# Attention values two units to a bank, and layer 3 with gelu and tanh read straight from PSUM

## The chip, the cores and the metric

One Trainium2 chip, one of its cores. The metric is the device time of one execution in microseconds (us); of a kernel's runs the median is taken. Three runs of the kernel before took 2492.44, 2498.31 and 2498.45 us.

## The reference

Four layers are applied one after the other to x, which holds 4 batches of 512 tokens with 512 channels in float32. A conditioning vector of 512 numbers per batch scales and shifts the normalised activations. Cut to what matters:

```python
# layer 0: layernorm, 16 heads of 32 with windowed keys from a latent, projection
# layer 1: rms norm, 8 query heads of 64 over one key head; then a gated MLP of 2048
# layer 2: layernorm, 16 heads of 32, normalised q and k; then an MLP of 2048 with tanh-gelu
# layer 3, eight experts of 64 channels each, side by side:
xr = x.reshape(Bx, Tx, 8, 64)
h = jax.nn.gelu(jnp.einsum('btel,elf->btef', xr, W1) + b1, approximate=False)
y = (jnp.einsum('btef,efl->btel', h, W2) + b2).reshape(Bx, Tx, Dx)
hn = _layernorm(y, ln_g, ln_b) * (1.0 + scale) + shift
return x + jax.nn.silu(hn) @ out_W + out_b
```

In each attention layer the scores pass a softmax and are then multiplied by the values.

## The kernel before, in words

All matmuls are float32. The kernel's author writes stages as Python generators and runs two of them side by side: side A (`AttentionSide`, line 427) and side M (`OtherSide`, line 463). A stage is a kind and a batch: `a01` is the attention of layers 0 and 1, `a2` that of layer 2, `m1` the MLP of layer 1, `m2` the MLP of layer 2 followed by layer 3, `mlp2` that MLP alone, and `half0` and `half1` are layer 3 for tokens 0 to 255 and 256 to 511 of the last batch. The lists `STREAM_A` and `STREAM_M` (line 98) say which stage each side takes in which order. At the start both sides have an `a01`; from then on an attention stage of one batch stands beside an MLP stage of another; at the end `half1` is left alone.

The order of the instructions is set before the program runs, by a planner. `Clocks` (line 161) keeps a model of when every tile is written and every engine is free. A stage yields `Until(...)` when its next piece needs something; `interleave` (line 1576) picks, among the pieces whose wait is over by the model, the one whose stage is furthest behind, and notes its instructions. At the end all noted instructions are emitted in the order of their modelled start. So a change of one stage's pieces moves the instructions of both sides, and nothing is reordered on the chip: each engine works through its own list and waits on semaphores.

All instructions of DVE, ACT and POOL are issued at line 301, all matmuls at line 354 (`mm`), all transposes at line 360 (`tr`). PSUM holds three pairs: two tiles of two banks each, called `two` (line 330), used for attention scores, and two single banks for each side, called `bank`. `evict` (line 376) copies a bank to SBUF on ACT or DVE, whichever the model frees first.

Attention (line 745) goes unit by unit. A unit is 128 queries of one group of heads: 16 units in layers 0 and 2, and 8 in layer 1. `scores` makes one unit's scores in two `two` tiles; DVE finds maxima, ACT exponentiates, POOL divides by the sum; `back` transposes the probabilities on PE and evicts them to `pT` tiles (side A) or `hid` (side M); `values` (lines 988, 1082 and 1220, one for each layer) multiplies them by v. The finished units wait in the list `late`:

```python
            if len(late) == 2:
                yield Until(*when, side.at, of=late[0][1])
                values(*late.pop(0))
                cost += work[1]
```

So the values of unit i-2 run when unit i is about to be transposed. Value products of layers 0 and 2 use 32 columns of the PE array and four of them run side by side in the four column groups (the profile writes the stationary shape 128*32), those of layer 1 use 64 (128*64). The scores use 32 or 64 rows (32*128, 64*128). All other large products and the transposes use the whole array (128*128).

Layer 3 is `experts` (line 1291). For each of four pairs of experts, `first` multiplies 64 channels by w1 (64*128), in two steps f of two products; after each step DVE adds the bias to one half and ACT to the other, and after both one gelu runs over the whole `hid` tile. `second` multiplies by w2 (128*64), DVE adds b2, `third` transposes back to y. Then `norm` takes mean and variance of each token's 512 values with one `bn_stats` and one `bn_aggr`, POOL raises the variance to the power -1/2, DVE scales, `turned` transposes and applies gain and lift (half the chunks on ACT, half on DVE), one silu runs over all of hT, and the products with `out3` follow.

Of the kernel before, what the change touches and what calls it, by code (L numbers as in the profile page):

```python
# [19 lines left out]
P = 128  # L20
# [288 lines left out]
def cond_seq_kernel(ctx: ExitStack, tc: tile.TileContext, a: dict, out: bass.AP):  # L309
# [17 lines left out]
    def name(s):  # L327
        return f"{s}_{next(uid)}"
# [310 lines left out]
        for _ in norm_steps(*args, **kw):  # L639
            pass  # L640

    def norm_steps(n, src, eps, rms=False, tiles=range(NT)):

        mv, own = tiny([P, NT, 2], "mv"), slice(tiles[0], tiles[-1] + 1)
        for t in tiles:
            st = tiny([P, 6], "st")
            vector.bn_stats(st, src[:, t, :])
# [97 lines left out]
    def attention(side, units, scores, back, values, work, first, final=True):  # L745

        def scorable():  # L750
            return max(locked[0], clocks.free("two", 2, 2))

        def later(rest):
            locked[0] = math.inf

            def then():
                locked[0] = 0.0
                rest()

            return then  # L760

        yield Until(scorable, of=first)
        (p, rest), late = scores(units[0]), []
        rest()
        yield work[0]
        for i, u in enumerate(units):
            cost, more = 0.0, i + 1 < len(units)
            when = [scorable] if more else []
            if len(late) == 2:
                yield Until(*when, side.at, of=late[0][1])  # L770
                values(*late.pop(0))
                cost += work[1]
            else:
                yield Until(*when)
            nxt, rest = scores(units[i + 1]) if more else (None, None)
            side.open = final and i + 2 >= len(units)

            if more:
                rest = later(rest)
            yield cost + (work[0] if more else 0.0)  # L780
            pT = yield from back(u, p, rest)
            late.append((u, pT))
            p = nxt
        for u, pT in late:
            yield Until(side.at, of=pT)
            values(u, pT)
            yield work[1]

    def turn_full(side):
        def back(u, p, then):  # L790
# [95 lines left out]
    def attention0(b, side):  # L886
# [98 lines left out]
                yield 0.45  # L985
            return [pT]

        def values(u, pT):
            c, qt = u
            (pT,), o, bl = pT, side.bank(), blocks(qt)  # L990
            for i, (at, n) in enumerate(bl):
                for g in range(4):
                    mm(
                        o[quarter(g), 0:P], lhsT=v[0:n, qt, i, quarter(g)],
                        rhs=pT[0:n, i, g * P : (g + 1) * P], start=i == 0, stop=i == len(bl) - 1,
                    )
            evict(ctxT[:, c, qt * P : (qt + 1) * P], o[:, 0:P])

        if "1" not in tabs:

# [10 lines left out]
    def attention1(b, side):  # L1011
# [67 lines left out]
            soft(0)  # L1079
            return p, lambda: soft(1)  # L1080

        def values(u, pT):
            c2, qt = u
            o = side.bank().rearrange("p (i q) -> p i q", q=P)
            for i in range(2):
                for at in range(NT):
                    for j in range(2):
                        mm(
                            o[half(j), i, :], lhsT=v[:, at, :], rhs=pT[i][:, j, at, :],
                            start=at == 0, stop=at == NT - 1,  # L1090
                        )
            evict(ctxT[:, 2 * c2 : 2 * c2 + 2, qt * P : (qt + 1) * P], o[:, 0:2, :])
# [70 lines left out]
    def attention2(b, side):  # L1163
# [9 lines left out]
        for which, dst in (("q2", qT), ("k2", kT)):  # L1173
            unit = side.ring.take(which)
            for t in range(NT):
                ps = yield from by_token(side, t, hT, unit)
                q, sq = side.t1(), side.t2()
                if which == "q2":
                    vector.tensor_tensor(q, ps, qb, ALU.add)
                else:  # L1180
                    vector.tensor_copy(q, ps)
                scalar.activation(sq, q, AF.Square)
                ss, inv = tiny([P, 16], "ss"), tiny([P, 16], "inv16")
                vector.tensor_reduce(ss, sq.rearrange("p (h d) -> p h d", d=32), axis=AX.X, op=ALU.add)
# [32 lines left out]
            soft(0)  # L1217
            return p, lambda: soft(1)

        def values(u, pT):  # L1220
            c, qt = u
            o = side.bank()
            for at in range(NT):
                for g in range(4):
                    mm(
                        o[quarter(g), 0:P], lhsT=v[:, at, c * P + 32 * g : c * P + 32 * g + 32],
                        rhs=pT[g // 2][:, g % 2, at, :], start=at == 0, stop=at == NT - 1,
                    )

            vector.tensor_scalar(ctxT[:, c, qt * P : (qt + 1) * P], o[:, 0:P], vb[:, c : c + 1], None, ALU.add)  # L1230
# [60 lines left out]
    def experts(b, side, tiles=range(NT)):  # L1291
# [11 lines left out]
        w1 = unit[:, 0:1024].rearrange("p (c f) -> p c f", f=256)  # L1303
        w2 = unit[:, 1024:2048].rearrange("p (e f l) -> p e f l", f=2, l=64)
        y = side.n()

        def first(p):
            hid = side.hid()
            per = 4 // len(hid)

            def at(j, f):
                return hid[2 * j // per][:, (2 * j + f) % per, 0:n]

            for f in range(2):
                yield Until(side.pair_at, of=[xT[:, p, lo : lo + n], w1])
                s = side.pair()
                for j in range(2):
                    r = slice(64 * j, 64 * j + 64)
                    mm(
                        s[j][:, 0:n], lhsT=w1[r, p, f * P : (f + 1) * P], rhs=xT[r, p, lo : lo + n],  # L1320
                        start=True, stop=True,
                    )
                for j in range(2):
                    bias = V_B1 + 4 * p + 2 * j + f
                    if j == 0:
                        vector.tensor_scalar(at(j, f), s[j][:, 0:n], vec[:, bias : bias + 1], None, ALU.add)
                    else:
                        scalar.activation(at(j, f), s[j][:, 0:n], AF.Identity, bias=vec[:, bias : bias + 1])
                yield 1.2 * n / S
            for h in hid:  # L1330
                scalar.activation(h[:, :, 0:n], h[:, :, 0:n], AF.Gelu)
            return at

        def second(p, at):
# [13 lines left out]
        def third(p, yT):  # L1348
            yield Until(side.at, of=[yT[:, 0:n]])
            ps = side.bank()  # L1350
            for t in range(len(tiles)):
                tr(ps[:, t * P : (t + 1) * P], yT[:, t * P : (t + 1) * P], ident)
            evict(y[:, tiles[0] : tiles[-1] + 1, p * P : (p + 1) * P], ps[:, 0:n].rearrange("p (t n) -> p t n", n=P))
            yield 0.45 * n / S

        hid = yield from first(0)
# [8 lines left out]
                t = tiles[p]  # L1365
                gpsimd.tensor_tensor(xs[b][:, t, :], xs[b][:, t, :], ob, ALU.add)
        yield from third(*late)
        norm(y, y, 1e-5, tiles=tiles)
        hT = side.late()
        yield from turned(side, y, hT, b, coefs["gain"], coefs["lift"], tiles)  # L1370
        side.open = side.clear = side is sideM
        scalar.activation(hT[:, :, lo : lo + n], hT[:, :, lo : lo + n], AF.Silu)
        for t in tiles:
            ps = yield from by_token(side, t, hT, unit3)
            if n < S:
# [16 lines left out]
    def conditioning(side):  # L1392
# [93 lines left out]
        vector.tensor_tensor(gain, e1, col(V_LNG), ALU.mult)  # L1486
        vector.tensor_tensor(lift, e1, col(V_LNB), ALU.mult)
        vector.tensor_tensor(lift, lift, coefs["e2"], ALU.add)
        yield 1.0
        bias2.append(buf("late"))  # L1490
        load(bias2[0], a["bias"].rearrange("(t p) k -> p t k", p=P))
# [197 lines left out]
```

## Time and profile before

| What | Value |
|---|---|
| runs | 2492.44, 2498.31, 2498.45 us |
| profiled execution, its own time | 2497.25 us |
| its span, first to last instruction | 2495.5 us |
| granted TensorE clock over the span | 0.992 |
| activation table loads on ACT (39) | 50.0 us |
| gelu over 128x2048 (with the silu of the full stages, 27) | 1.911 us each |
| biased copy of a bank on ACT, 128x512 | 0.681 us each |
| bias added from a bank on DVE, 128x512 | 0.746 us each |
| bn_stats over 128x512 (DVE) | 0.685 us each |

PE is TensorE's matmul row, PEld its weight loads, DVE VectorE, ACT ScalarE, POOL GpSimd. A group is written as line, engine, operation, output and inputs, shape and count. For a matmul the first shape is that of the stationary operand, so a group with 128*32 uses 32 columns of the array. Matmuls are pipelined: the length of one (0.27 us for 128 columns, 0.6 us for 512) is its latency, and what it costs in a row of many is the distance from its start to the next start.

### The profile page before, as it was taken

The numbers are of one execution on the slowest core, as the hardware profiler recorded it, in microseconds if no ns is written. First come the engines' busy times: TensorE is split into PE (matmuls) and PEld (weight loads), VectorE is DVE, ScalarE is ACT, GpSimd is POOL, SyncE is SP. The second block draws the span as 40 slices with busy tenths as digits, with TensorE's granted clock in tenths as the row PEclk, the third lists the DMA queues.
The fourth block names the chain that finished last, engine by engine and source line by source line (L and its number), as shares of the span: only waits on it lengthen the run. The fifth ranks groups of instructions, "written<-read, shape, count | busy, mean of one in ns | idle before, by whom it ended". The sixth has DMA issues, their size and how long they took to land.

```text
span 2495.5 us, 33420 instructions
## 1 busy us (share of the span) xinstructions
PE 2432.5 (97%) x12564; PEld 1242.0 (50%) x12564; DVE 1190.5 (48%) x3180; ACT 877.6 (35%) x2071; POOL 733.5 (29%) x921
## 2 busy tenths in 40 slices
PE   7989999999999999999999999999999999999997
PEld 4555655444554555554455455554455444554443
DVE  6766552133654454625554455443465333763233
ACT  2645441002551351414353043333255202651233
POOL 2433320005332223324222232424332205533221
PEclk9999999999999999999999999999999999999998
DMA  3220122220113111111211111112111221102210
GB/s 112 100 74 18 52 68 68 86 87 34 35 52 106 51 52 55 39 68 55 89 48 61 63 69 65 42 56 72 68 35 52 83 89 53 44 32 95 72 55 21
DMA packets 83312, 154.18 MB, mean 62 GB/s; under 512 B 3584, under 2 KB 10784, under 8 KB 83152
## 3 DMA queue, kind: packets, MB, share of 16 engines
q1 hardware_dynamic: 82544, 151.83, 17.9%
q8 instruction: 100, 1.64, 0.3%
q14 instruction: 60, 0.49, 0.1%
q0 software_dynamic: 176, 0.15, 0.1%
q10 hardware_dynamic: 432, 0.07, 0.0%
HBM read 147.83 MB, written 4.21 MB: 61 GB/s over the span
## 4 chain that ended last, share of the span: by engine, by line
PE 88%; DVE 3%; issue 3%; ACT 2%; POOL 2%; DMA 1%; ACTq 0%; POOLq 0%; DVEq 0%
PE bank L354 71%; PE bank L360 11%; PE two L354 6%; POOL inv L301 1%; ACT probs L301 1%; DVE probs L301 1%; ACT wm L301 0%; DVE neg L301 0%; POOL t L301 0%; DVE pT L301 0%; DMA late_ada_g<-in_units 0%; DMA wm<-in_units 0%; DVE t L301 0%; DMA late_ada_t<-in_units 0%; POOL probs L301 0%
## 5 line engine op out<-in xcount | busy, mean ns | idle before, releaser
L301 POOL TENSOR_SCALAR probs<-probs,inv 128x512 f32<-128x512 f32 (+4 forms) x544 | 316.4, 596 | 688.4 <-DVE inv L301 579.4
L301 ACT ACTIVATE probs<-probs,neg 128x512 f32<-128x512 f32 (+2 forms) x448 | 265.4, 594 | 254.8 <-DVE neg L301 254.3
L360 PEld LDWEIGHTS bank<-ident,probs 128*128 128x128 f32 (+2 forms) x1744 | 201.9, 141 | 161.9 <-issue 128.6
L360 PE MATMUL bank<-ident,probs 128*128 128x128 f32 (+2 forms) x1744 | 245.4, 276 | 4.1 <-ACT arow L301 1.2
L354 PE MATMUL bank<-mT,wm_gate 128*128 128x512 f32 x512 | 248.9, 597 | 0.0
L354 PE MATMUL bank<-mT,wm_up 128*128 128x512 f32 x512 | 245.7, 597 | 0.0
L354 PE MATMUL bank<-wm_down,hid 128*128 128x512 f32 x512 | 239.6, 596 | 0.7 <-DVE hid L301 0.7
L301 DVE CUSTOM_DVE_ANT_0 probs<-two,late 128x512 f32<-128x512 f32 x256 | 166.2, 686 | 74.3 <-PE two L354 56.4
L354 PE MATMUL bank<-wm_fc,hid 128*128 128x512 f32 x384 | 187.6, 594 | 0.0
L354 PE MATMUL bank<-mT,wm_fc 128*128 128x512 f32 x384 | 182.6, 597 | 0.0
L301 ACT COPY pT<-bank 128x512 f32<-128x512 f32 (+2 forms) x240 | 133.8, 580 | 83.8 <-PE bank L360 75.8
L354 PEld LDWEIGHTS bank<-pT,v 128*32 128x32 f32 (+2 forms) x3488 | 110.7, 116 | 95.9 <-issue 33.3
L354 PE MATMUL bank<-pT,v 128*32 128x128 f32 (+2 forms) x3488 | 146.0, 278 | 8.3 <-DVE pT L301 5.8
L301 ACT ACTIVATE mt<-bank 128x512 f32<-128x512 f32 x64 | 37.8, 591 | 327.6 <-PE bank L354 327.6
L354 PE MATMUL bank<-wa_q,h 128*128 128x512 f32 x320 | 152.4, 599 | 0.2 <-DVE t L301 0.2
L301 DVE TENSOR_TENSOR x<-x,bank 128x512 f32<-128x512 f32 x100 | 68.4, 684 | 176.1 <-PE bank L354 176.0
L354 PE MATMUL two<-kT,nq 32*128 32x512 f32 (+5 forms) x1088 | 150.0, 539 | 1.1 <-DVE mx L301 1.1
L354 PEld LDWEIGHTS bank<-wm_down,hid 128*128 128x128 f32 x512 | 91.7, 190 | 98.1 <-issue 96.2
L354 PEld LDWEIGHTS bank<-mT,wm_up 128*128 128x128 f32 x512 | 91.0, 190 | 98.2 <-issue 97.7
L301 DVE RECIPROCAL inv<-total 128x2 f32<-128x2 f32 x320 | 53.0, 166 | 172.9 <-ACT probs L301 155.7
L354 PEld LDWEIGHTS bank<-mT,wm_gate 128*128 128x128 f32 x512 | 90.0, 190 | 90.8 <-issue 90.3
L301 DVE COPY pT<-bank 128x512 f32<-128x512 f32 (+2 forms) x199 | 131.1, 680 | 5.9 <-PE bank L360 5.0
(221 smaller groups left out, 3396.3 us busy)
## 6 DMA issues: line engine op xcount, KB each, us to landing
wm_fc<-in_units SPq DMA_DIRECT2D x24, 1024.0 KB, 5.6
wm_gate<-in_units SPq DMA_DIRECT2D x16, 1024.0 KB, 5.7
wm_up<-in_units SPq DMA_DIRECT2D x16, 1024.0 KB, 5.7
wm_down<-in_units SPq DMA_DIRECT2D x16, 1024.0 KB, 5.4
wa_q<-in_units SPq DMA_DIRECT2D x10, 1024.0 KB, 5.5
wa_fc<-in_units SPq DMA_DIRECT2D x8, 1024.0 KB, 5.5
wa_o<-in_units SPq DMA_DIRECT2D x6, 1024.0 KB, 5.7
wa_k<-in_units SPq DMA_DIRECT2D x4, 1024.0 KB, 5.6
```

What stands on the lines that cost most here:

```text
L301: return call(*map(real, args), **{k: real(x) for k, x in kw.items()})
L354: latest[0] = nc.tensor.matmul(real(out), lhsT=real(lhsT), rhs=real(rhs), **kw)
L360: latest[0] = nc.tensor.transpose(real(out), real(src), unit)
```

## The change

Three things are changed.

Values: the list `late` is emptied two units at a time. One call of `values` writes both units' results beside each other into one bank, and one instruction evicts 256 columns where two evicted 128 each (twice that in layer 1). It waits for the pT tiles of both units. In the iterations between, no values run.

Layer 3: the bias is added inside the gelu, which reads PSUM directly, four times per pair of experts (each 128x512, or 128x256 in the halves). The banks come from `two`: both `two` tiles in a full stage, one in a half. Both steps f are one piece now. Each transposed chunk of y gets its `bn_stats` at once, 128 columns at a time, and `bn_aggr` reads four of them. silu(z) is written as (1 + tanh(z/2)) * z/2, with gain and lift halved beforehand: for each chunk ACT takes the tanh from the bank, DVE makes z/2 from the same bank, and DVE multiplies.

Layer 2: the copy of k's bank may go to ACT or DVE, where it was DVE's.

```diff
+    def norm_steps(n, src, eps, rms=False, tiles=range(NT), stats=None):
...
+            if stats is None:
+                st = tiny([P, 6], "st")
+                vector.bn_stats(st, src[:, t, :])
+            else:
+                st = stats[:, t, :, :]
             vector.bn_aggr(mv[:, t, :], st)
...
             if len(late) == 2:
-                yield Until(*when, side.at, of=late[0][1])
-                values(*late.pop(0))
-                cost += work[1]
+                yield Until(*when, side.at, of=late[0][1] + late[1][1])
+                values(late)
+                late = []
+                cost += 2 * work[1]
             else:
-                yield Until(*when)
+                yield Until(0.0, *when)
...
-        for u, pT in late:
-            yield Until(side.at, of=pT)
-            values(u, pT)
-            yield work[1]
+        yield Until(side.at, of=sum((pT for _, pT in late), []))
+        values(late)
+        yield len(late) * work[1]
...
+        def values(two):
+            o, (c, first) = side.bank(), two[0][0]
+            for k, ((_, qt), (pT,)) in enumerate(two):
+                bl = blocks(qt)
+                for i, (at, n) in enumerate(bl):
+                    for g in range(4):
+                        mm(
+                            o[quarter(g), k * P : (k + 1) * P], lhsT=v[0:n, qt, i, quarter(g)],
+                            rhs=pT[0:n, i, g * P : (g + 1) * P], start=i == 0, stop=i == len(bl) - 1,
+                        )
+            evict(ctxT[:, c, first * P : (first + 2) * P], o[:, 0 : 2 * P])
...
-                    vector.tensor_copy(q, ps)
+                    evict(q, ps)
...
+            yield Until(lambda: clocks.free("two", 2, 2 if n == S else 1), of=[xT[:, p, lo : lo + n], w1])
+            banks = [two_banks() for _ in range(2 if n == S else 1)]
...
+            for f in range(2):
                 for j in range(2):
                     bias = V_B1 + 4 * p + 2 * j + f
-                    if j == 0:
-                        vector.tensor_scalar(at(j, f), s[j][:, 0:n], vec[:, bias : bias + 1], None, ALU.add)
-                    else:
-                        scalar.activation(at(j, f), s[j][:, 0:n], AF.Identity, bias=vec[:, bias : bias + 1])
-                yield 1.2 * n / S
-            for h in hid:
-                scalar.activation(h[:, :, 0:n], h[:, :, 0:n], AF.Gelu)
+                    scalar.activation(at(j, f), bank(j, f), AF.Gelu, bias=vec[:, bias : bias + 1])
+            yield 2.2 * n / S
...
+            for t in tiles:
+                vector.bn_stats(stats[:, t, p, :], y[:, t, p * P : (p + 1) * P])
...
-        norm(y, y, 1e-5, tiles=tiles)
+        norm(y, y, 1e-5, tiles=tiles, stats=stats)
         hT = side.late()
-        yield from turned(side, y, hT, b, coefs["gain"], coefs["lift"], tiles)
+
+        own = slice(lo, lo + n)
+        for c in range(NC):
+            yield Until(side.at, of=[y[:, t, c * P : (c + 1) * P] for t in tiles])
+            ps, h, z = side.bank()[:, 0:n], hT[:, c, own], side.t1()[:, 0:n]
+            for i, t in enumerate(tiles):
+                tr(ps[:, i * P : (i + 1) * P], y[:, t, c * P : (c + 1) * P], ident)
+            gain, lift = (coefs[x][:, c, b : b + 1] for x in ("gain", "lift"))
+            scalar.activation(h, ps, AF.Tanh, bias=lift, scale=gain)
+            vector.tensor_scalar(z, ps, gain, lift, ALU.mult, ALU.add)
+            vector.scalar_tensor_tensor(h, h, 1.0, z, ALU.add, ALU.mult)
+            yield 0.45 * len(tiles) / NT
         side.open = side.clear = side is sideM
-        scalar.activation(hT[:, :, lo : lo + n], hT[:, :, lo : lo + n], AF.Silu)
...
+        for x in (gain, lift):
+            vector.tensor_scalar(x, x, 0.5, None, ALU.mult)
```

The `values` of layers 1 and 2 are changed in the same way as the one shown.

More of the change, by code (lines that the diff above doesn't have):

```diff
@@ L640, in norm @@
             pass
-    def norm_steps(n, src, eps, rms=False, tiles=range(NT)):
+    def norm_steps(n, src, eps, rms=False, tiles=range(NT), stats=None):
         mv, own = tiny([P, NT, 2], "mv"), slice(tiles[0], tiles[-1] + 1)
         for t in tiles:
-            st = tiny([P, 6], "st")
-            vector.bn_stats(st, src[:, t, :])
+            if stats is None:
[3 more added lines that the diff above has]
+                st = stats[:, t, :, :]
             vector.bn_aggr(mv[:, t, :], st)
@@ L986, in back @@
             return [pT]
[L988 to L997, printed above, removed]
+        def values(two):
[9 more added lines that the diff above has]
+            evict(ctxT[:, c, first * P : (first + 2) * P], o[:, 0 : 2 * P])
         if "1" not in tabs:
@@ L1080, in scores, with values @@
             return p, lambda: soft(1)
[L1082 to L1092, printed above, removed]
+        def values(two):
+            o, (c2, first) = side.bank().rearrange("p (i q) -> p i q", q=2 * P), two[0][0]
+            for k, (_, pT) in enumerate(two):
+                for i in range(2):
+                    for at in range(NT):
+                        for j in range(2):
+                            mm(
+                                o[half(j), i, k * P : (k + 1) * P], lhsT=v[:, at, :], rhs=pT[i][:, j, at, :],
+                                start=at == 0, stop=at == NT - 1,
+                            )
+            evict(ctxT[:, 2 * c2 : 2 * c2 + 2, first * P : (first + 2) * P], o)
         units = [(c2, qt) for c2 in range(2) for qt in range(NT)]
@@ L1218, in scores, with values @@
             return p, lambda: soft(1)
[L1220 to L1230, printed above, removed]
+        def values(two):
+            o, (c, first) = side.bank(), two[0][0]
+            for k, (_, pT) in enumerate(two):
+                for at in range(NT):
+                    for g in range(4):
+                        mm(
+                            o[quarter(g), k * P : (k + 1) * P],
+                            lhsT=v[:, at, c * P + 32 * g : c * P + 32 * g + 32],
+                            rhs=pT[g // 2][:, g % 2, at, :], start=at == 0, stop=at == NT - 1,
+                        )
+            rows = slice(first * P, (first + 2) * P)
+            vector.tensor_scalar(ctxT[:, c, rows], o[:, 0 : 2 * P], vb[:, c : c + 1], None, ALU.add)
         units = [(c, qt) for c in range(NC) for qt in range(NT)]
@@ L1305, in experts @@
         y = side.n()
+        if ("stats", b) not in shared:
+            shared["stats", b] = clocks.tile("stats", 1, small, (P, NT, NC, 6), "stats", name("stats"))
+        stats = shared["stats", b]
         def first(p):
@@ L1312, in at, with bank @@
                 return hid[2 * j // per][:, (2 * j + f) % per, 0:n]
+            yield Until(lambda: clocks.free("two", 2, 2 if n == S else 1), of=[xT[:, p, lo : lo + n], w1])
+            banks = [two_banks() for _ in range(2 if n == S else 1)]
+            def bank(j, f):
+                return banks[f][:, j, :] if n == S else banks[0][:, j, f * n : (f + 1) * n]
             for f in range(2):
-                yield Until(side.pair_at, of=[xT[:, p, lo : lo + n], w1])
-                s = side.pair()
                 for j in range(2):
@@ L1319, in first @@
                     mm(
-                        s[j][:, 0:n], lhsT=w1[r, p, f * P : (f + 1) * P], rhs=xT[r, p, lo : lo + n],
+                        bank(j, f), lhsT=w1[r, p, f * P : (f + 1) * P], rhs=xT[r, p, lo : lo + n],
                         start=True, stop=True,
                     )
+            for f in range(2):
                 for j in range(2):
                     bias = V_B1 + 4 * p + 2 * j + f
-                    if j == 0:
-                        vector.tensor_scalar(at(j, f), s[j][:, 0:n], vec[:, bias : bias + 1], None, ALU.add)
-                    else:
-                        scalar.activation(at(j, f), s[j][:, 0:n], AF.Identity, bias=vec[:, bias : bias + 1])
-                yield 1.2 * n / S
-            for h in hid:
-                scalar.activation(h[:, :, 0:n], h[:, :, 0:n], AF.Gelu)
+                    scalar.activation(at(j, f), bank(j, f), AF.Gelu, bias=vec[:, bias : bias + 1])
+            yield 2.2 * n / S
             return at
```

## The prediction

> **What bounds the kernel.** I read the page first (busy shares and the chain that ended last), then the busy time by stretches, then the PE timeline of one attention unit, then who PE waited for in each stretch. The page, its busy line and its chain:
>
> ```profile
> PE 2432.5 (97%) x12564; PEld 1242.0 (50%) x12564; DVE 1190.5 (48%) x3180; ACT 877.6 (35%) x2071; POOL 733.5 (29%) x921
> ...
> PE 88%; DVE 3%; issue 3%; ACT 2%; POOL 2%; DMA 1%; ACTq 0%; POOLq 0%; DVEq 0%
> ```
>
> The next view gives each stretch's length, then busy us of PE, PEld, DVE, ACT, POOL, the granted clock, DMA share and GB/s:
>
> ```profile
> 0.00:400.00 400.00, 361.95 (x2634) 217.66 (x2635) 242.54 (x786) 183.91 (x557) 131.55 (x239) 0.98 0.20 66
> 400.00:2380.00 1980.00, 1969.61 (x9587) 979.06 (x9586) 906.19 (x2314) 654.82 (x1459) 579.40 (x663) 1.00 0.18 63
> ...
> 2440.00:2495.50 55.50, 41.50 (x168) 19.17 (x166) 21.27 (x43) 20.80 (x35) 5.20 (x5) 0.84 0.07 24
> ```
>
> From 400 to 2380 us PE stands still for only 1980.0 - 1969.6 = 10.4 us: there the time is the sum of what PE does, and DVE and ACT, at 46% and 33%, only have to keep up. At the start PE idles 38 us and in the last 55 us 14 us, and there the clock is 0.84.
>
> A busy PE may still lose time between instructions, so I looked at one unit of layer 2's attention in the PE timeline (start, length, group; a float32 product makes two records, a transpose one):
>
> ```profile
> 1281.34 0.60 PE L360 MATMUL bank<-ident,probs 128*128 128x128 f32 x4
> 1281.78 1.02 PE L354 MATMUL bank<-mT,wm_gate 128*128 128x512 f32 x2
> 1282.64 0.60 PE L360 MATMUL bank<-ident,probs 128*128 128x128 f32 x4
> 1283.17 1.08 PE L354 MATMUL bank<-pT,v 128*32 128x128 f32 x32
> 1284.18 1.14 PE L354 MATMUL two<-kT,nq 32*128 32x512 f32 x8
> 1285.25 3.70 PE L354 MATMUL bank<-mT,wm_up 128*128 128x512 f32 x8
> ```
>
> Read start to start. Four transposes before a full product take 0.44 us (0.109 each), but 0.53 before the values: 0.09 is lost on leaving the 128*128 shape. The values run four side by side, 8 steps of 0.109 = 0.87, and take 1.01: 0.14 lost. The scores should take as long as one full product (0.86, from 1281.78 to 1282.64) and take 1.07: 0.21 lost. The same reading in layer 1 (1030.66, 1032.56, 1034.48 us) gives 0.15 for 128*64 values and 0.20 for 64*128 scores. So every change of PE's shape has a price, and it is paid on the engine that bounds.
>
> **Part 1, values of two units in one bank.** No matmul is added or removed: both programs have 7,674. What changes is how often the shape does. Counted in the PE order of the two built programs, by the shape that is left:
>
> - 128*128: 257 before, 206 after, at 0.093 us: 23.9 to 19.2
> - 32*128 (scores): 127 to 128, at 0.213: 27.1 to 27.3
> - 128*32 (values): 146 to 86, at 0.139: 20.3 to 12.0
> - 64*128 (scores, layer 3 first product): 69 to 50, at 0.20: 13.8 to 10.0
> - 128*64 (values, layer 3 second): 64 to 48, at 0.153: 9.8 to 7.3
>
> That is 664 changes to 519, and 94.9 to 75.8 us: **19.1 us less PE time**. (Prices are the medians of such steps over the whole trace; the rows above are instances.) By place: 3.6 us before 400 us, 13.7 from 400 to 2440, 1.8 in the tail.
>
> [...]
>
> What it costs. Values of units i-2 and i-1 now start together, right after unit i-1 was transposed, where before they ran one unit later. From the PE order, with the row times above, the PE work between a unit's last transpose and its first value product falls: the median from about 10.6 us to 6.4 in the middle, the shortest to 2.2 there and to 1.4 before 400 us. The evictions (pT copy, 0.58 us on ACT, 0.68 on DVE) end in the middle 0.7 us (median) to 2.3 (worst) after the transposes, in the start up to 3.1, as ACT's copies show. So in the middle almost all stay hidden: I add 1 us. In the start, where PE already waits for these copies,
>
> ```profile
> PE bank L354 <- DVE pT L301: 6.7, 4, 2.7
> PE bank L354 <- ACT pT L301: 3.3, 4, 1.6
> PE bank L354 <- DVE hid L301: 2.9, 3, 2.0
> ```
>
> two stages of 12 pairs each could wait. Bounds: nothing, and one DVE copy for each of 24 pairs, 24 x 0.68 = 16 us. I take 3, nearer the low end because each side's work covers the other's. Behind a waiting value product stand all later PE instructions of both sides; then scores, DVE maxima and exp come late. Fewer, wider evictions (layer 2: 64 of 0.344 us become 32 of about 0.48, the row for 128x256) save DVE 6.5 us off the path: nothing. The layer-2 k copy, now given to ACT or DVE, likewise.
>
> **Part 2, layer 3 in full stages (batches 0 to 2).** Per pair of experts, ACT did two biased copies (0.68) and a gelu over 2,048 columns (1.91), 3.3 us; now four gelus from the banks, 4 x 0.68 = 2.7. DVE loses two 0.75 adds. Chunked statistics cost DVE four short bn_stats for one of 0.685; a 128x128 DVE copy takes 0.28, so 1.1 us. silu of 2,048 columns (1.91) and its table load (1.28; 39 loads become 34) become four tanh (0.78), four more DVE scalings (0.81) and four products (0.68). All this lies beside PE in the middle; what can reach PE is order. A pair's first products now take both "two" buffers, and the next pair's wait until four gelus have read them, 2.7 us plus a table load the first time; between them PE has one second product (1.87) and four transposes (0.44). So 0.4 to 1 us can show per pair, 12 pairs: up to +8. Against that, the row
>
> ```profile
> PE bank L360 <- POOL t L301: 6.0, 4, 2.0
> ```
>
> is k or q waiting for POOL's scaling just here (1127 and 1168 us), where the new order puts other products: down to -6. I take 0.
>
> [...]
>
> **Part 3, the tail.** The last half stage is alone, and its chain is serial:
>
> ```profile
> PE bank L360 <- DVE nq L301: 3.9, 1, 3.9
> PE bank L354 <- ACT h L301: 3.1, 1, 3.1
> PE two L354 <- DVE pT L301: 1.9, 1, 1.9
> PE bank L354 <- ACT hid L301: 0.7, 1, 0.7
> ```
>
> ```profile
> 2479.11 1.28 ACT L301 ACT_TABLE_LOAD   x1 [0.49 <-DVE h L301]
> 2480.40 1.06 ACT L301 ACTIVATE h<-h 128x1024 f32<-128x1024 f32 x1
> ```
>
> The first wait spans copy, two bn_stats with aggregates (1.9 us), POOL's pow, scaling. With three of four chunks counted early, two short stats (0.28), two aggregates (0.18) and var (0.17) make 1.1: -0.8. Table load and silu, 2.34 us, go; in their place DVE does eight operations of 256 columns (0.54 and about 0.42), 3.8 us from the first transpose where the old way took 4.75 (-0.9), and PE can begin with chunk 0 (I count 0.2): -1.1. In the new PE order the last fc2 products of batch 3 stand inside the first half's chain, so its two waits (1.9, 0.7) are covered; but the last x tile must pass DVE and POOL (0.69 + 1.27) before its transpose, with little PE work between: +1.6. The last eight products took 10.1 us for 8 x 0.86, at the low clock after the waits; with a wait left I keep that. Sum -3, with its 1.8 us of shape changes -4.8; bounds 0 and -10.
>
> **Sum.** Start -3.6 + 3, middle -13.7 + 1, full stages 0, tail -4.8: -18.1. The profiled execution took 2497.25 us (span 2495.5), so 2479; the median shown, 2498.31, is 1 us above it and I take them as one.
>
> **Rivals.**
> 1. The waits eat it: the start loses the full 16 us and the full stages 8 more than I take, 2497 - 18 + 13 + 8 = 2500, no change. For: DVE runs at 61% before 400 us. Against: the stages' order leaves at least 1.4 us of cover. 0.09.
> 2. Slower: layer 3's "two" buffers. Scores of the other side use the same two buffers. If attention units ran beside the 12 pairs, each would wait four gelus (2.7 us) and PE with it: 33 us, 2479 + 33 = 2512. It decides from 7 of 12 pairs on. Against: at 1120 to 1195 us the other side does q, k and v products (wa_q, wa_k, wa_v in the timeline), no scores. 0.06.
> 3. More: the POOL waits go and the tail gains 10: 2479 - 6 - 5 = 2468 or less. 0.12.
> 4. The count falls but the price stays (a merged block refills as long as two): only part 3 is left, about 2494. Against: inside a values block the steps hold 0.109 through. 0.03.
> Forecast, 2469 to 2489: 0.70.
>
> A measurement here tells no less than 0.3% (7.5 us) from no change: faster ends at 2490.8, slower begins at 2505.8. Faster 0.70 + 0.12 = 0.82, same 0.09 + 0.03 = 0.12, slower 0.06. Range 2467 to 2490: forecast and the third case, and the near part of the first.
>
> **What would show it.** Right: 664 - 519 shape changes gone, PE busy near 2414, PE idle in the middle near 10 us, value groups of 64 records with the lost 0.14 once; no table load between the last transposes and the last products. Wrong: PE waiting for pT or hid beyond 400 us, first products of layer 3 waiting for ACT, scores waiting for layer 3's gelu.

## The result and the profile after

The kernel after took 2480.03 us (median of 6 runs, 2476.6 to 2482.74), the kernel before 2494.9 in 6 runs: ratio 0.9941, 95% interval 0.9926 to 0.9955, 14.9 us less. The forecast was 2479.0. The profiled execution took 2482.74 us, its span 2481.0; that of before took 2497.25, so the two traces differ by 14.5 us.

The page of the kernel after, its busy line and its chain:

```profile
PE 2418.9 (97%) x12564; PEld 1254.5 (51%) x12564; DVE 1177.2 (47%) x3174; ACT 856.1 (35%) x2053; POOL 737.9 (30%) x921
...
PE 91%; DVE 3%; ACT 3%; DMA 1%; issue 1%; POOL 0%; ACTq 0%; POOLq 0%; DVEq 0%
```

The number of PE records is the same, and PE is busy 13.6 us less. PE's share of the chain rose from 88% to 91%: it is still the bound.

The stretches of the kernel after (length, busy us of PE, PEld, DVE, ACT, POOL, granted clock, DMA share, GB/s):

```profile
0.00:400.00 400.00, 364.72 (x2632) 221.88 (x2633) 238.46 (x776) 184.40 (x544) 132.58 (x239) 0.95 0.20 66
400.00:2365.00 1965.00, 1954.27 (x9602) 985.93 (x9601) 903.44 (x2325) 644.30 (x1454) 582.59 (x664) 1.00 0.18 63
...
2425.00:2481.00 56.00, 43.06 (x169) 20.72 (x168) 21.62 (x53) 15.69 (x36) 7.71 (x7) 0.92 0.07 24
```

PE idles 1965.0 - 1954.3 = 10.7 us in the middle, as before. In the start it idles 35 us where it idled 38, but its clock is 0.95 where it was 0.98.

One value group of layer 2 in the PE timeline of the kernel after (start, length, group):

```profile
1278.44 2.74 PE L354 MATMUL bank<-mT,wm_up 128*128 128x512 f32 x6
1281.11 1.96 PE L354 MATMUL bank<-pT,v 128*32 128x128 f32 x64
1283.00 1.14 PE L354 MATMUL two<-kT,nq 32*128 32x512 f32 x8
```

The group now has 64 records. From its start to the next it takes 1.89 us, which is 16 steps of 0.109 and once 0.15. Before, 32 records took 1.01, with 0.14 lost: two units paid it twice.

**An account of all PE time.** I gave each product of the PE order the distance it has in an undisturbed row of its own kind (0.858, 0.432 or 0.218 us for 512, 256 or 128 columns, 0.109 for a transpose, divided by the number that run side by side), added the prediction's price at each change of shape, and called what is left of the measured distances the rest: waits, what is lost behind them, and a low clock. Stretches are cut by work done, so they hold equal work: the start is the first 340 us of products, the middle ends at 2200.

| Stretch | before: us = changes + rest | after | change predicted | measured |
|---|---|---|---|---|
| start | 423.5: 25.5 + 57.8 | 424.5: 22.0 + 62.4 | -3.6 + 3 | -3.5 + 4.6 |
| middle | 1963.0: 64.0 + 38.4 | 1945.9: 50.7 + 34.5 | -13.7 + 1 | -13.3 - 3.9 |
| tail | 94.8: 5.4 + 18.8 | 96.5: 3.1 + 22.9 | -1.8 - 3 | -2.3 + 4.1 |

The sum is -14.4 us, the difference of the two traces but for rounding. The total came out near the forecast, but from a middle that gained more and a tail that lost where a gain was expected.

The tail's waits of PE in the kernel after, 2365 us to the end (total, times, longest):

```profile
PE two L354 <- ACT hid L301: 3.2, 3, 1.9
PE bank L360 <- DVE nq L301: 2.9, 1, 2.9
PE bank L360 <- POOL x L301: 2.0, 1, 2.0
PE two L354 <- ACT pT L301: 1.8, 3, 0.6
```

The wait for nq fell from 3.9 to 2.9, the 3.1 us for the silu is gone, the x tile's wait came as expected. But the first and the last row are new: products into `two` that wait for ACT, six times, 5.0 us. The prediction had no term for them.

### The profile page after: what moved, and what is told of

It reads as the page before. It is cut to its first block, busy times and chain, and to the rows that moved or that the text cites. A ratio compares the mean times of both kernels' runs of the same rounds, so it can differ in the third digit from the quotient of the medians.

```text
span 2481.0 us, 33372 instructions
## 1 busy us (share of the span) xinstructions
PE 2418.9 (97%) x12564; PEld 1254.5 (51%) x12564; DVE 1177.2 (47%) x3174; ACT 856.1 (35%) x2053; POOL 737.9 (30%) x921
## 4 chain that ended last, share of the span: by engine, by line
PE 91%; DVE 3%; ACT 3%; DMA 1%; issue 1%; POOL 0%; ACTq 0%; POOLq 0%; DVEq 0%
PE bank L354 73%; PE bank L360 11%; PE two L354 7%; ACT probs L301 1%; DVE probs L301 1%; ACT wm L301 1%; DVE neg L301 0%; DVE mx L301 0%; DMA wa_q<-in_units 0%; DMA late_ada_s<-in_units 0%; DVE t L301 0%; DMA wm<-in_units 0%; ACT hid L301 0%; DVE wm L301 0%; DVE pT L301 0%
## 5 line engine op out<-in xcount | busy, mean ns | idle before, releaser
L301 DVE COPY pT<-bank 128x512 f32<-128x512 f32 (+2 forms) x217 | 143.0, 680 | 11.4 <-PE bank L360 10.7
L301 ACT COPY pT<-bank 128x512 f32<-128x512 f32 (+3 forms) x222 | 123.7, 581 | 67.5 <-PE bank L360 59.7
L354 PE MATMUL bank<-pT,v 128*32 128x128 f32 (+2 forms) x3488 | 131.9, 277 | 0.3 <-DVE pT L301 0.3
```

What stands on the lines that cost most here:

```text
L301: return call(*map(real, args), **{k: real(x) for k, x in kw.items()})
L354: latest[0] = nc.tensor.matmul(real(out), lhsT=real(lhsT), rhs=real(rhs), **kw)
```

## The experiments

Each run had its own runs of the kernel before beside it: 2495.23, 2493.49 and 2494.44 us in three groups of four kernels. The table has the median, its ratio to those, and the account of its profiled execution. One trace's rest can't be read closely: eight kernels with pairs have the same PE order through the start, and their rests there run from 55.6 to 62.4; three with values one by one also share an order there and have 51.9 to 57.8. In the middle the kernel after and half_two_tiles have one order, and 34.5 and 37.8.

| Kernel | us | ratio, 95% interval | changes | rest: start, middle, tail |
|---|---|---|---|---|
| before | 2494.9 | | 663 | 57.8, 38.4, 18.8 |
| after | 2480.03 | 0.9941, 0.9926 to 0.9955 | 518 | 62.4, 34.5, 22.9 |
| values_alone | 2486.99 | 0.9959, 0.9944 to 0.9975 | 568 | 61.8, 40.1, 17.0 |
| layer3_alone | 2490.04 | 0.9977, 0.9966 to 0.9987 | 613 | 55.3, 35.4, 23.1 |
| z_first | 2476.52 | 0.9922, 0.9907 to 0.9937 | 518 | 59.6, 34.2, 19.5 |
| half_two_tiles | 2470.86 | 0.99, 0.9883 to 0.9917 | 519 | 58.8, 37.8, 13.4 |
| both_mends | 2470.51 | 0.9899, 0.9885 to 0.9914 | 519 | 58.5, 35.4, 12.6 |
| two_banks_in_a_row | 2486.89 | 0.9969, 0.9957 to 0.998 | 523 | 63.4, 37.2, 22.8 |
| dummy_between_units | 2509.14 | 1.0057, 1.0045 to 1.0069 | 647 | 59.8, 37.6, 21.0 |
| dummy_behind_units | 2500.09 | 1.0022, 1.0014 to 1.0031 | 575 | 63.0, 38.7, 22.9 |
| start_one_by_one | 2472.24 | 0.9909, 0.9895 to 0.9922 | 546 | 51.9, 37.8, 15.3 |
| silu_table_back | 2472.95 | 0.9914, 0.9899 to 0.9928 | 519 | 55.8, 35.2, 17.5 |
| stats_back | 2468.33 | 0.9898, 0.9881 to 0.9916 | 521 | 55.6, 34.8, 12.3 |
| k_on_vector | 2476.37 | 0.9922, 0.9909 to 0.9936 | 519 | 61.2, 38.2, 15.7 |

### values_alone and layer3_alone: the two parts apart

The first is the kernel before with the new `late` and the three new `values`; the second is the kernel after with the old ones.

```diff
-                yield Until(*when, side.at, of=late[0][1])
-                values(*late.pop(0))
+                yield Until(*when, side.at, of=late[0][1] + late[1][1])
+                values(late)
```

> The kernel before with part 1 alone (values of two units in one bank). Theory (each change of PE's shape has its price, by the shape left): 664 changes become 568, 94.9 us become 82.5, so 12.4 us less: about 2482.5 against 2494.9. Rival (the new waits for the younger unit's pT eat it, and the gain measured lies in layer 3 and the tail): 2492 or more.

> The changed kernel with the values of each unit apart again (parts 2 and 3 alone). 664 changes of shape become 613, 88.2 us, so 6.7 us less by shapes. Theory: the layer-3 order gives back most of that in waits for ACT, since the whole change gained 14.9 and the values should account for 12.4: about 2492. Rival (layer 3 gains what the prediction gave it, 6.7 by shapes and 3 in the tail): 2485.

The values alone gained 8.2 us, the rest of the change 5.2. The first lies between its theory and its rival. For the values the account says -12.4 for 95 fewer changes, +4.0 of rest in the start, +1.7 in the middle and -1.8 in the tail: -8.5. What the 12.4 us lack is, in this trace, mostly the start. Layer 3 alone has 50 changes fewer (-6.7) and 4.3 us more rest in the tail; its median lies between theory and rival, and its profiled execution, 2489.3 us, agrees with neither better. That this part also saves changes (its two steps f are one piece) was in the prediction's count; without this run the saving would pass for one of the values.

### half_two_tiles: what the tail lost

```diff
-            yield Until(lambda: clocks.free("two", 2, 2 if n == S else 1), of=[xT[:, p, lo : lo + n], w1])
-            banks = [two_banks() for _ in range(2 if n == S else 1)]
+            yield Until(lambda: clocks.free("two", 2, 2), of=[xT[:, p, lo : lo + n], w1])
+            banks = [two_banks() for _ in range(2)]
...
-                return banks[f][:, j, :] if n == S else banks[0][:, j, f * n : (f + 1) * n]
+                return banks[f][:, j, 0:n]
```

> The changed kernel, but the half stages of layer 3 put their two steps into two tiles of two banks, as the full stages do. Theory (PE's last product of a pair waits for ACT's gelu because both use one tile): the six waits of 0.56 to 1.9 us, 5.0 us in all, go, but a pair's first products then wait for all four gelus of the pair before, some 0.3 us each: about 2477. Rival (the wait moves in full to the next pair): 2480.

It gained 9.2 us, more than either. The kernel after, PE timeline of the first pair of experts in the first half:

```profile
2409.66 1.13 PE L354 MATMUL two<-mT,wm_exp 64*128 64x256 f32 x6
2412.69 1.56 PE L354 MATMUL two<-mT,wm_exp 64*128 64x256 f32 x10 [1.90 <-ACT hid L301]
2414.18 3.68 PE L354 MATMUL bank<-wa_fc,pT 128*128 128x512 f32 x4
```

The same place with two tiles:

```profile
2409.46 1.13 PE L354 MATMUL two<-mT,wm_exp 64*128 64x256 f32 x8
2410.52 2.84 PE L354 MATMUL bank<-wa_fc,pT 128*128 128x512 f32 x6
2413.29 1.14 PE L354 MATMUL two<-mT,wm_exp 64*128 64x256 f32 x8
```

Three products (six records) run, and the fourth waits for ACT's first gelu, behind a table load of 1.28 us. In the built program that gelu stands ahead of the fourth product, and the product has a wait on it. The gelu reads the first bank of the tile and the product writes the second, so no bank is shared: the wait is kept for the tile as a whole, as I read the program. With one tile for each f there is nothing to wait for.

The waits are 5.0 us; what was lost is more. From 2409.66 to 2414.18 the eight products take 4.52 us and not 1.93 (8 x 0.216 and one change of 0.20), and the two full products behind them 1.83 and 1.78 us for 0.86 each. The clock in these four us and in the four before:

```profile
2410.00:2414.00 4.00, 2.10 (x16) 1.41 (x12) 0.00 (x0) 2.34 (x4) 3.50 (x3) 1.00 0.09 27
2414.00:2418.00 4.00, 4.00 (x8) 1.33 (x8) 0.00 (x0) 2.09 (x6) 0.00 (x0) 0.57 0.00 0
```

So a wait of 1.90 us cost 4.4: 2.6 at the wait and 1.8 behind it, at a clock of 0.57. Five more such waits, of 0.5 to 0.6 us, cost 1.2 to 1.3 each. Together 10.9 us of the tail's rest are of this kind in the kernel after, 1.2 with two tiles.

### z_first and both_mends: two engines read one bank

```diff
-            scalar.activation(h, ps, AF.Tanh, bias=lift, scale=gain)
             vector.tensor_scalar(z, ps, gain, lift, ALU.mult, ALU.add)
+            scalar.activation(h, z, AF.Tanh)
```

The second kernel has this and the two tiles of the halves.

> The changed kernel, but DVE makes z/2 from the bank first and ACT takes the tanh of that from SBUF, so that one engine alone reads the bank. Theory (two readers of one bank take turns and hold it, so the next transposes wait): the 4.6 us that transposes wait for ACT in the full stages and about 1.5 us of the last chain go: about 2474. Rival (the bank is not what is waited for, DVE is): no change, 2480.

> The kernel after with both mends of layer 3: z is made on DVE from the bank and ACT takes the tanh of z, so that only one engine reads the bank; and the halves put their two steps f into two tiles, as the full stages do. Theory (the two waits lie in different places, the bank's two readers in the last chain of each stage and the halves' shared tile in their first products, and add): 2480.0 - 3.5 - 9.2 = 2467. Rival (both mends shorten one and the same chain of the tail, and the larger hides the smaller): 2470.9, as with two tiles alone.

The prediction let z run on DVE beside the tanh on ACT. In the kernel after they take turns. ACT in a full stage, and PE, which waits for the same bank:

```profile
1156.28 2.30 ACT L301 ACTIVATE hid<-bank,coef_lift,coef_gain 128x512 f32<-128x512 f32 x3 [0.91 <-DVE mt L301]
```

```profile
1155.42 0.66 PE L360 MATMUL bank<-ident,mn 128*128 128x128 f32 x4 [1.28 <-ACT hid L301]
1157.11 0.65 PE L360 MATMUL bank<-ident,mn 128*128 128x128 f32 x4 [1.03 <-ACT hid L301]
```

ACT waits for DVE's reading (0.91 us; mt is the z of a full stage), and PE's next transposes wait until both have read (1.28 and 1.03 us). In the built program the second reader depends on the first; no run here lets the two read at once, so what that would take is not shown.

The middle's waits for these banks in the kernel after, and then with one reader:

```profile
PE bank L360 <- ACT hid L301: 4.6, 4, 1.3
```

```profile
PE bank L360 <- DVE mt L301: 3.0, 4, 1.0
```

They are 3.0 us for 4.6, and the last chain is 0.7 us shorter. The median fell by 3.5 us, nearer to the theory's number than to the rival's, but the intervals of both ratios overlap. On top of the two tiles the same edit gave 0.4 us, so the rival's number came there: the two mends do not add. In the account of z_first the middle's rest fell by only 0.3 us, the tail's by 3.4, and the start's by 2.8, though the order there is unchanged. One reader is worth between 0 and 3.5 us, and these runs don't settle where.

### two_banks_in_a_row: order or bank

```diff
-                yield Until(*when, side.at, of=late[0][1] + late[1][1])
+                yield Until(*when, lambda: side.at(2), of=late[0][1] + late[1][1])
...
-            o, (c, first) = side.bank(), two[0][0]
-            for k, (_, pT) in enumerate(two):
+            for (c, qt), pT in two:
+                o = side.bank()
```

> The kernel after, but the two units whose values run back to back go into a bank each and are evicted one by one, as before; each side has two single banks and both must now be free. The shape changes become 523, worth 76.3 us by the prediction's prices (519 and 75.8 in the kernel after), and the evictions double again in number. Theory (the gain comes from the order of the products, not from the shared bank): 2480 to 2482. Rival (the shared bank with its wider eviction is what pays, by fewer evictions and free banks): 2487 and more, as the 8 us that the values alone brought would go.

The rival's number came, within 0.1: 2486.89, 6.9 us more, so my theory that the order alone pays in full falls. What the order does alone is seen against layer3_alone, which has the same layer 3 and the old values: the middle takes 1948.6 us for 1955.7, 7.1 less, but the start 426.1 for 420.9, 5.2 more. With the shared bank the middle is the same (1945.6 to 1949.6 us in the kernel after, in z_first and in the six on two tiles), and the start takes 417.7 to 424.5 in the eight kernels named above, whose pairs share a bank. So the rival is right in the time, but the place isn't shown. The middle lies inside the range of kernels with a shared bank, which speaks for the order alone there. The start is 1.6 us above their highest and about 5 above their mean, which would fit a side that must wait for both its banks, as the edit's first lines have the planner do; but that range is 7 us wide for one and the same order. No run parts the wider eviction from the freed bank.

### dummy_between_units and dummy_behind_units: the price itself

```diff
+                if k == 0:
+                    tr(o[:, 3 * P : 4 * P], ident, ident)
```

after the inner loop over a unit's blocks; the second kernel has `k == 1`. The transposed identity goes to columns that nobody reads.

> The kernel after with one product more for each pair of units in layers 0 and 2: a 128x128 transpose of the identity into columns that nobody reads, between the first unit's values and the second's, 64 in all. It makes 647 shape changes of 519, worth 90.8 us of 75.8 by the prediction's prices. Theory (shape changes cost what the prediction says): 15.0 us for the changes and 64 x 0.109 = 7.0 for the transposes, 2480 + 22 = 2502. Rival (what costs is not the change of shape): 7 us for the transposes alone, 2487.

> The same 64 transposes, but behind the second unit's values, where a change of shape mostly follows anyway: 575 shape changes, worth 81.1 us. Theory: 5.3 us for the changes and 7.0 for the transposes, 2492. Rival (what costs is not the change of shape): 2487, the same as with the transposes between the units. The two runs differ by 10 us in the theory and by nothing in the rival.

The two hold the same 64 instructions and differ by where they stand. They differ by 9.05 us where the price of 72 changes says 9.7 and the rival nothing. So a change of shape costs about what the rows said. The PE timeline of the first kernel shows the price itself:

```profile
1291.23 1.08 PE L354 MATMUL bank<-pT,v 128*32 128x128 f32 x32
1292.24 0.33 PE L360 MATMUL bank<-ident 128*128 128x128 f32 x1
1292.50 1.08 PE L354 MATMUL bank<-pT,v 128*32 128x128 f32 x32
1293.51 1.14 PE L354 MATMUL two<-kT,nq 32*128 32x512 f32 x8
```

Each unit's values take 1.01 us again, so the 0.14 is paid twice. The level is off: the two are 7 and 8 us above the theory. The same lines hold a part of it. The lone transpose takes 0.26 us to the next product, where 0.109 and a price of 0.093 make 0.20. That is the median of all 64 in the first kernel, and of the 56 before scores in the second: 64 x 0.056 = 3.6 us, and 3.2.

The account takes the prices as given: between the units it has +15.0 for changes, +7.0 for transposes and -1.5 of rest, behind them +5.3, +7.0 and +4.9. By that rest the two profiled executions differ by only 3.3 us. The one of the first kernel took 2503.36 us, near the theory, while five others took 2507 to 2510 without a profile; where those spent it stays open.

### start_one_by_one: does it pay in the start

```diff
+            elif len(late) == 2:
+                yield Until(*when, side.at, of=late[0][1])
+                values([late.pop(0)])
+                cost += work[1]
```

for the attention of layers 0 and 1 in batches 0 and 1, on top of the two tiles in the halves.

> The kernel after with two tiles in the halves (2470.9 us), but the first two attention stages of layers 0 and 1, those of batches 0 and 1 that fill the start, take their units' values one by one as before. 546 shape changes for 519, 3.5 us more by the prediction's prices; what the start loses beyond products and changes was 57.9 us before and about 60 with the units in pairs. Theory (in the start the longer waits give back about 2.5 of the 3.5 us): 2472. Rival one (they give back more than pairs save there, so pairs don't pay in the start): 2469 or less. Rival two (pairs cost nothing in the start): 2474.5.

2472.24 against 2470.86: as the theory had it, and less than can be told from nothing. The clock from 100 to 150 us shows where the start gives back. In this kernel:

```profile
100.00:150.00 50.00, 43.50 (x493) 27.80 (x483) 37.02 (x201) 35.73 (x139) 24.34 (x60) 0.93 0.38 128
```

In the kernel after:

```profile
100.00:150.00 50.00, 43.38 (x436) 29.13 (x432) 31.16 (x175) 33.03 (x125) 21.33 (x53) 0.76 0.33 115
```

PE is busy equally long and gets fewer instructions done. On two tiles, the base of this run, the clock there is 0.87 with 472 records. Three kernels with values one by one in the start have 0.93 here; the others, with pairs, 0.73 to 0.90.

### silu_table_back, stats_back and k_on_vector: the small parts

All three stand on half_two_tiles, with one edit of the change undone:

```diff
-            scalar.activation(h, ps, AF.Tanh, bias=lift, scale=gain)
...
+        scalar.activation(hT[:, :, lo : lo + n], hT[:, :, lo : lo + n], AF.Silu)
```

```diff
-                vector.bn_stats(stats[:, t, p, :], y[:, t, p * P : (p + 1) * P])
...
-        norm(y, y, 1e-5, tiles=tiles, stats=stats)
+        norm(y, y, 1e-5, tiles=tiles)
```

```diff
-                    evict(q, ps)
+                    vector.tensor_copy(q, ps)
```

> The kernel after with two tiles in the halves, but layer 3 transposes, scales and applies one silu over all of hT as before, and gain and lift are not halved. Theory (only the last half's chain is on the path: from its first nq transpose to its first product 5.7 us passed before and 4.2 with tanh): 2470.9 + 1.5 = 2472.4. Rival (table load and silu, 1.3 + 1.9 us, also reach PE in the three full stages and in the first half): 2476 or more.

> The kernel after with two tiles in the halves, but the statistics of layer 3 are taken over 512 columns at the end as before, not by chunks. 521 shape changes for 519. Theory (only the last chain is on the path: PE waits there 3.2 us between the last transposes of y and the first of nq, and 4.1 us before): 2470.9 + 0.9 + 0.3 = 2472.1. Rival (the short statistics stand in DVE's queue ahead of work that PE waits for in the full stages, and taking them away gains): 2469 or less.

> The kernel after with two tiles in the halves, but layer 2's copy of k's bank is always DVE's as before. Theory (nothing waits for it): 2470.9, within a microsecond. Rival (the k products wait for a free bank, and the choice between ACT and DVE was what freed it): 2473 or more.

**silu_table_back**, 2472.95, fits the theory (2472.4), though its interval also covers half_two_tiles. The last chain with the silu:

```profile
2450.59 0.91 PE L360 MATMUL bank<-ident,nq 128*128 128x128 f32 x4 [2.94 <-DVE nq L301]
...
2456.12 6.29 PE L354 MATMUL bank<-wm_out,h 128*128 128x512 f32 x7 [3.07 <-ACT h L301]
```

and with tanh, in the kernel after:

```profile
2463.64 0.91 PE L360 MATMUL bank<-ident,nq 128*128 128x128 f32 x4 [2.94 <-DVE nq L301]
2465.57 0.69 PE L360 MATMUL bank<-ident,nq 128*128 128x128 f32 x2 [1.02 <-DVE t L301]
2466.62 0.69 PE L360 MATMUL bank<-ident,nq 128*128 128x128 f32 x2 [0.36 <-ACT h L301]
2467.66 9.41 PE L354 MATMUL bank<-wm_out,h 128*128 128x512 f32 x16 [0.35 <-DVE t L301]
```

5.5 us to the first product, and 4.0 (4.2 in half_two_tiles): one wait of 3.07 became three short ones. The tail's rest is 4.1 us above half_two_tiles: beside this chain's 1.4, the same eight last products took 10.15 us where they took 8.56 there.

**stats_back**, 2468.33, missed the theory and hit the rival's side, though its interval covers half_two_tiles. On the last chain the theory is right: the wait for nq is 3.9 us again, 1.0 more. It is given back elsewhere: the x tile's wait of 2.0 us in the tail is gone, and the middle's 4.6 us for `hid` are 0.6, with 2.6 for POOL t in their place. So short statistics gain 1.0 us where they were aimed and no measured time in all.

**k_on_vector** took 5.5 us more, on the rival's side, though the two intervals overlap. But the account does not lay it to the copy: the middle, where k is copied, has 38.2 us of rest against 37.8. The difference is 2.4 in the start and 2.3 in the tail, and there the two kernels have the same PE order (the first 3,743 and the last 2,009 instructions of 7,674); in the tail six records of `wm_out` products stand 0.71 to 0.85 us apart where they stood 0.43 or 0.53, which makes the 2.3 us. I take it for a spread between executions and not for an effect of k, but only these two traces speak for that.

The lowest time is that of stats_back, 0.9898; half_two_tiles (0.99) and both_mends (0.9899) can't be told from it. All three beat the kernel after by about 10 us.

## Why the prediction was right, and where it was wrong

1. **Bound and price: right.** The same five prices go with 345 to 446 changes in the middle of fourteen kernels and leave a rest of 34.2 to 40.1 us, while the priced part moves from 50.7 to 64.0. Two kernels that differ in place alone differ by 9.05 us for 9.7. (The prediction's five rows add up to 663 and 518, as in the traces, and not to its 664 and 519; the difference is 145 either way.) PE busy is 2418.9, not near 2414; with two tiles it is 2413.4, so the 5 us are mostly the tail's slow products. Rival 4 (count without price) is out.
2. **Start, -3.6 + 3: sum about right, mechanism wrong.** The rest grew by 4.6. These two traces alone couldn't show it, but the eight kernels with pairs average 59.2 and the three without 55.0, 4.2 less. So in the start the pairs gain next to nothing. But PE did not wait longer for pT or hid. Their three rows, 12.9 us together before, are down to this one and 0.7 us for ACT's pT:

```profile
PE bank L354 <- DVE pT L301: 3.8, 3, 2.1
```

What is late is PE itself, at a lower clock (0.76 from 100 to 150 us, where before had 0.93); why it is lower with pairs is not shown. Rival 1 (16 us of waits) is out.

3. **Middle, +1: too high by 5 in these traces.** The 6.0 us for POOL t are 0.3, replaced by 4.6 us for the bank with two readers. PE's idle time is the same, 10.7 us for 10.4, so the 3.9 us of rest that went are not waits; the same order left 34.5 and 37.8 in two executions, so most of it can be spread. The waits of layer 3's first products that I feared, 0.4 to 1 us for 12 pairs, did not come, and rival 2 (scores waiting for gelus) is out: no product into `two` waits in the middle. That rival's "7 of 12 pairs" was also miscounted: at 2.7 us each it takes ten to reach 2505.8.
4. **Tail, -4.8: wrong in sign, +1.7.** Its listed terms held: statistics -0.9 for -0.8, silu -1.7 for -1.1, the two waits of 1.9 and 0.7 covered, x 2.0 for 1.6. (The silu's 4.75 us were counted from ACT's first reading of a bank and not, as the prediction says, from the first transpose; from there it was 5.7, and is now 4.0.) The step that failed is the one that priced layer 3's first products: it counted the `two` buffers of the full stages and gave the halves nothing, though the section on the change says that a half takes one tile for both steps f. That was 10.9 us, and 9.2 came back when it alone was mended. Without it the tail would have gained 7 to 8 us, inside the prediction's bounds.
5. **The case "more" (2468 or less)** did not come, but both its steps were there: the POOL wait went, and the tail's gain stood behind the halves' shared tile.

The total, 2480.0 for 2479.0, thus owes something to luck: +1.6, -4.4 and +6.5 us of errors by place. It owes more to the base: the forecast took 18.1 us from 2497.25, but the median before is 2494.9 over six runs, and 14.9 us came off. The lower base hid 2.3 of the 3.2 us that were missing.

## What to carry to other kernels

Where PE is the bound, count the changes of its array shape in the PE order and price each by the shape it leaves (0.093 to 0.213 us in these traces); running products of one shape for two units back to back was here worth most of what the count says (the values alone gained 8.2 us of 12.4, and next to nothing of it in the start). When a new instruction reads a tile that PE still writes, look in the built order for a reader that comes between two writes: one tile for each step removed a wait of 1.90 us that cost 4.4. And before giving two engines one bank to read at the same time, count them one after the other, as DVE and ACT took turns here (ACT waited 0.91 us).

## What was not expected of the hardware

- A short wait of PE cost nearly as much again behind it. After 1.90 us of wait two full products took 1.83 and 1.78 us instead of 0.86, at a clock of 0.57; after the tail's 2.9 us wait for nq and the short waits behind it the first product took 1.87.
- It was not the same in two executions. The kernel after and the one with two tiles in the halves have the same PE order for the first 7,547 of 7,674 instructions. Behind the same two waits in the middle (1.28 and 1.03 or 1.04 us) three full products took 2.58 us in the first, at a clock of 1.00, and 4.27 in the second, at 0.60, and the middle's rest is 34.5 and 37.8. First the kernel after, then the one with two tiles; the group behind these starts at 1160.62 and 1158.81:

```profile
1158.04 2.74 PE L354 MATMUL bank<-wa_k,h 128*128 128x512 f32 x6
```

```profile
1154.54 4.44 PE L354 MATMUL bank<-wa_k,h 128*128 128x512 f32 x6
```

  Why the clock fell in one and not in the other is not shown.
- Statistics over 128 columns took 0.28 us each, 0.49 for two in a row and about 0.87 for four, where one over 512 took 0.685: cheaper than the 1.1 that I took from a 128-column copy.
